# A message-passing layer on one core: another order of the step, slots found earlier, smaller last segments, the second bias by ScalarE

## The chip, the cores and the metric

The kernel runs on one core of one Trainium2 chip. The metric is the device time of one execution in microseconds (us). TensorE (PE) does matrix products, VectorE (DVE) and ScalarE (ACT) work elementwise, GpSimd (POOL) issues the indirect DMAs here, SyncE (SP) issues the plain ones. PSUM is the accumulator that TensorE writes, in banks of 128 partitions by 512 f32 words; SBUF is the on-chip memory; the tables named below lie in DRAM.

## The reference

`x` is 12500 nodes by 128 features. There are 412500 edges with a source, a target (sorted by target), 20 attributes and a weight.

```python
h    = relu(layernorm(x)) @ W_in2f
Wij  = (ssp(edge_attr @ W_f1 + b_f1) @ W_f2 + b_f2) * edge_weight[:, None]
agg  = segment_sum(h[dst] * Wij, src, 12500)
out  = x + ssp(agg @ W_o1 + b_o1) @ W_o2 + b_o2       # ssp(v) = softplus(v) - log 2
```

The edges are sorted by `dst`, so a run of edges reads few rows of h; the sum goes by `src`, which is in no order. That sum is what shapes the kernel.

## The kernel before, in words

**Chunks.** The edges are cut into 806 chunks of 512 (`CH`), each of four tiles of 128 (`QT`); four chunks make a group, 202 groups in all. For every chunk the kernel forms the 512 x 128 messages and POOL sends them by four indirect DMAs (one per tile, L795, "scatter") into rows ("slots") of a table in DRAM. The slots of a table are laid out by blocks of 128 source nodes (98 blocks), so that a later pass can load all messages of one block and add them up by products with a one-hot matrix. In each slot the 129th word is the node's place within its block.

**Slots.** Which slot an edge takes is its rank among the edges of its block so far. `blocks` (L673, VectorE) makes the one-hot of the blocks (128 x 392), `rank` (L692 and, to pass the count on, L725) multiplies it with a triangle of ones into one PSUM bank that is kept for this, `free`; `rank_end` takes the maximum over the blocks (`top`, L697, VectorE), and three small steps on VectorE make row numbers of it (L717 to L721). Ranks are made six chunks ahead of the chunk whose messages are sent (`LR` = 6).

**Messages.** For chunk k: SP loads the 32 rows of h that it reads (`rows`, table h3, three bf16 parts, tile `near`); VectorE makes the one-hot `at` (`window`, L744); TensorE multiplies them (`pick`, L772, into `picked`); ScalarE scales that by the edge weight (`picked`, L780, `hg`, four instructions). Beside it, for two chunks at a time, TensorE makes z = f W_f1 (`hidden`, L653), ScalarE Abs (L656), Exp (L657) and Ln (L662, `hidden_log`), and VectorE joins them to `r` (`hidden_end`, L668): that is the softplus. ScalarE copies the constant b_f1-and-b_f2 term into a PSUM bank (`bias`, L757), TensorE adds r W_f2 onto it in eight passes (`value`, L764, `v`). VectorE multiplies o = v hg (`message`, L791), and POOL scatters o. `v` and `picked` share three PSUM banks.

**Sums.** The groups are cut into segments (`SEGS` = 88, 40, 30, 14, 14, 8 and 8 groups), each with its own table. Once a segment's chunks are sent, `Collect` goes through its table in units of up to six tiles (`UT`): `load` by SP (tile `m`, L833), `compare` on VectorE (L844, one-hot `to`), `add` on TensorE (L857, into `acc`, a bank for four blocks, a "quad"), `keep` (L878 by ScalarE for the first segment, L880 by VectorE for the others, into `agg`, which stays in SBUF). With T tiles per block of 16, 8, 6, 3, 3, 2 and 2 (one more in a few blocks) that makes 4066 tiles in 824 units. All segments but the last are collected beside the chunks that follow; from the first segment's end (chunk 352) on, each step has some units, paced by planned due times (L995 to L1035).

**The order.** `step(k)` (L940 to L985) writes the order of each engine's work by hand, and no scheduler changes it. Its order for chunk k is: loads; blocks (k+7), end of the pair's softplus, window (k+2), message (k), keep; value and pick (k+1), bias (k+2), picked (k+1); compares; rank, hidden (k+4), log, add, tops. Clears of the slots (L1099, DMAs by SP) and the preparation of h (`make_h`, 25 quads of four node tiles) run beside the steps.

**Start and tail.** Ahead of the first chunk the kernel loads constants and makes h of the first four node tiles (`make_h(0)`), whose own table `tables[0]` serves the first chunks. After the last scatter come the rest of the units, the last segment's 206 tiles, and `finish` for each quad: z_out (L414), Abs and Relu (L385, L386), Exp and Ln (L394, L395), their sum (L420), x + b_o2 (L423), v_out (L427), the last add (L431) and the store (L434). The tail runs these parts of successive quads side by side.

Of the kernel before, what the change touches and what calls it, by code (L numbers as in the profile page):

```python
# [22 lines left out]
SEGS = (88, 40, 30, 14, 14, 8, 8)  # L23
# [6 lines left out]
UT = 6  # L30
# [6 lines left out]
def ceil_div(a, b):  # L37
    return -(-a // b)
# [3 lines left out]
def gnn_kernel(  # L42
# [38 lines left out]
    class Segment:  # L81
# [4 lines left out]
        def __init__(self, k):  # L86
# [7 lines left out]
            mean = (SEGS[k] * TG * P - (own[1] - own[0])) / QT * P / N  # L94
# [32 lines left out]


    tables = [(0, QN)]
# [4 lines left out]
    for c in range(NC):  # L134
        n = c * CH * N // n_edges
        table_of.append(0 if n < QN - NEAR - P else min(n // QN, NQ - 1) + 1)
# [4 lines left out]
    bf1, nbf1, bo1 = (sbuf(n, [P, 1]) for n in ("bf1", "nbf1", "bo1"))  # L141
# [10 lines left out]
    bf12 = sbuf("bf12", [P, P])  # L152
    zero = sbuf("zero", [P, ZR * RW])
# [27 lines left out]
    def load_x(q):  # L181
        n = min(QT, NTILE - q * QT)
        full = min(n, N // P - q * QT)
        xb = ln.tile([P, QT, P], F32, name="xb")
        if full < n:
            nc.vector.memset(xb[:, full:n, :], 0.0)
            nc.sync.dma_start(xb[:N % P, full, :], x[q * QN + full * P:N, :])
        if full:
            nc.sync.dma_start(xb[:, :full, :], x[q * QN:q * QN + full * P, :]
# [61 lines left out]

    def constants():
# [3 lines left out]
        first_load(0)  # L256
        nc.sync.dma_start(win, w_in2f)

        for j in range(NCHUNK):
            nc.sync.dma_start(wf1[32 * j:32 * j + RBF, :], w_f1)  # L260

        nc.scalar.preload_act_table_set("natural_log_exp_and_others")
        nc.scalar.dma_start(bf1, b_f1[:, None])
        nc.scalar.dma_start(wf2, w_f2)
        nc.scalar.dma_start(bf2, b_f2[None, :].to_broadcast([P, P]))
        make_identity(nc, ident)
        for _ in bounds(0, nc.gpsimd):
            pass

        prow_i = early_room[:WP, rows_at + 5 * NC:rows_at + 5 * NC + 1].bitcast(I32)  # L270
# [6 lines left out]
                                pattern=[[1, P]], channel_multiplier=-1)  # L277
        nc.gpsimd.memset(zero, 0.0)
# [8 lines left out]
        nc.vector.memset(bad, 0.0)  # L287
        nc.vector.memset(rel[:, NPART - 1, :], 0.0)
        nc.vector.memset(ones, 1.0)
        nc.vector.memset(none, 0.0)  # L290

        for t in range(QT):
            nc.vector.memset(turn[:, :, t:t + 1], -1.0 if t % 2 else 1.0)
        nc.vector.tensor_scalar(prow_i, prow_i, 7, None, op0=ALU.logical_shift_right)
        nc.vector.tensor_copy(prow, prow_i)
# [3 lines left out]

    def biases(psum):  # L300
# [911 lines left out]
```

## Time and profile before

| what | value |
|---|---|
| time, median of 13 runs | 5758.44 us (5727.84 to 5780.44) |
| the profiled execution's own time | 5751.31 us |
| its span | 5749.6 us |
| granted TensorE clock, mean | 0.726 of full speed |
| TensorE busy (weight loads) | 3837.9 us, 67% (2884.0 us, 50%) |
| VectorE busy | 3381.9 us, 59% |
| ScalarE busy | 2715.2 us, 47% |
| GpSimd busy | 3101.1 us, 54% |
| DMA | 820.80 MB, mean 143 GB/s |

By stage, from the busy time of each engine in three stretches:

| stretch, us | what runs | TensorE | VectorE | ScalarE | GpSimd | clock |
|---|---|---|---|---|---|---|
| 144 to 2416 | chunks alone | 1241 | 1152 | 1112 | 1282 | 0.62 |
| 2416 to 5608 | chunks and sums | 2387 | 2032 | 1466 | 1744 | 0.79 |
| 5608 to 5750 | sums and finish | 118 | 110 | 62 | 0 | 0.94 |

How to read the lines that follow. A group's line gives source line, engine, operation, the tiles it writes and reads, and a count; then busy us and the mean ns of one; then the engine's idle time just before these instructions, and what ended most of it. "issue" means that the profile shows nothing the engine waited for; "remote" that it was released by a semaphore whose sender the profile does not tell. A line of waits gives who waits for whom, the sum in us, the number of waits and the longest one (or, for issue, the sum, the count and the longest). A line of the timeline gives the start in us, the duration, engine, line, operation, tiles, and in brackets the idle time before it.

### The profile page before, as it was taken

To read this page: it belongs to the slowest core of one execution; us is meant where nothing else is said; L and a number is where in the kernel's file an instruction comes from. 1 tells how busy PE (TensorE), PEld (TensorE's weight loads), DVE (VectorE), ACT (ScalarE), POOL (GpSimd) and SP (SyncE) were. 2 spreads that over 40 slices of the span, in tenths; PEclk is the share of its full clock that TensorE was granted. 3 is DMA by queue.
4 is the path that set the end of the run, shared out by engine and by line. 5 is a ranking of instruction groups with operands and counts; after the bars stand their busy time and mean duration, and the time that the engine had idled before them with its cause. 6 is when DMAs were issued, how large, how long until landed. Compare 5 with 4: busy or idle time off the path is not lost. (4 is left out here: it accounts for less than half of the span.)

```text
span 5749.6 us, 71871 instructions
## 1 busy us (share of the span) xinstructions
PE 3837.9 (67%) x21576; PEld 2884.0 (50%) x21576; DVE 3381.9 (59%) x6726; ACT 2715.2 (47%) x5490; POOL 3101.1 (54%) x3244
## 2 busy tenths in 40 slices
PE   6555555655555555467777777777777777677778
PEld 4333333433333333356656566665656666555567
DVE  6555555555444444466665656666666666676767
ACT  5455555545444444444444444444444444444444
POOL 5555655655555555555555555555555555555550
PEclk7666666656665656678777778787877878787879
DMA  5444444443333333355664555655555556545547
GB/s 157 132 128 147 132 130 130 132 121 101 100 89 90 99 106 94 82 151 159 182 190 133 156 154 148 186 174 152 159 171 178 166 146 186 171 139 154 140 127 216
DMA packets 515581, 820.80 MB, mean 143 GB/s; under 512 B 177074, under 2 KB 312870, under 8 KB 515186
## 3 DMA queue, kind: packets, MB, share of 16 engines
q1 hardware_dynamic: 411586, 602.85, 37.4%
q0 software_dynamic: 103168, 213.15, 11.3%
q8 instruction: 176, 2.88, 0.2%
q14 instruction: 219, 1.79, 0.1%
q10 hardware_dynamic: 432, 0.13, 0.0%
HBM read 419.09 MB, written 396.64 MB: 142 GB/s over the span
## 5 line engine op out<-in xcount | busy, mean ns | idle before, releaser
L795 POOL DMA_INDIRECT slots<-o,slot x3224 | 3097.9, 961 | 2506.4 <-DVE o L791 1603.1
L764 PE MATMUL v<-wf,r 128*128 128x128 f32 x6448 | 1195.0, 342 | 561.8 <-issue 222.4
L857 PEld LDWEIGHTS acc<-to,m 128*128 128x128 f32 x8132 | 1237.8, 236 | 594.0 <-issue 281.8
L857 PE MATMUL acc<-to,m 128*128 128x128 f32 x8132 | 1332.1, 327 | 294.2 <-DVE agg L880 155.1
L780 ACT ACTIVATE hg<-picked,rcut 128x128 f32<-128x128 f32 x3224 | 913.0, 365 | 1276.1 <-remote 801.9
L764 PEld LDWEIGHTS v<-wf,r 128*128 128x128 f32 x6448 | 1066.4, 249 | 877.0 <-issue 332.0
L697 DVE TENSOR_REDUCE top<-free 128x4 f32<-128x392 f32 x806 | 451.3, 560 | 1622.4 <-remote 847.0
L757 ACT ACTIVATE v<-bf 128x512 f32<-128x512 f32 x804 | 478.1, 595 | 1196.6 <-DVE o L791 846.8
L653 PE MATMUL z<-f,wf 20*128 20x512 f32 x1612 | 654.6, 862 | 411.8 <-DVE r L668 238.0
L844 DVE TENSOR_TENSOR to<-count_ps,m 128x512 f32<-128x512 f32 (+3 forms) x824 | 644.6, 805 | 246.6 <-remote 111.3
L772 PE MATMUL picked<-near,at 96*128 96x128 bf16 x3224 | 391.6, 255 | 478.4 <-ACT hg L780 328.1
L668 DVE SCALAR_TENSOR_TENSOR r<-z,nbf,a 128x1024 f32<-128x1024 f32 x403 | 516.2, 1281 | 243.3 <-ACT a L662 128.4
L656 ACT ACTIVATE a<-z,bf 128x1024 f32<-128x1024 f32 x403 | 454.1, 1127 | 376.7 <-remote 282.4
L772 PEld LDWEIGHTS <-at 96*128 96x128 bf16 x3224 | 311.5, 117 | 540.5 <-issue 513.7
L791 DVE TENSOR_TENSOR o<-v,hg 128x512 f32<-128x512 f32 x806 | 547.8, 680 | 16.1 <-ACT hg L780 12.2
L744 DVE TENSOR_TENSOR at<-count_ps,rel 96x512 bf16<-96x512 f32 x806 | 545.3, 677 | 0.0
L653 PEld LDWEIGHTS z<-f,wf 20*128 20x128 f32 x1612 | 172.4, 236 | 629.2 <-issue 457.3
L662 ACT ACTIVATE a<-a,half 128x1024 f32<-128x1024 f32 x403 | 468.1, 1161 | 0.0
L673 DVE TENSOR_TENSOR inb<-count_ps,blk 128x392 f16<-128x392 f32 x806 | 445.7, 554 | 0.0
L657 ACT ACTIVATE a<-a 128x1024 f32<-128x1024 f32 x403 | 425.9, 1057 | 12.8
L725 PE MATMUL free<-inb,rest_of 128*128 128x392 f16 x806 | 331.9, 412 | 102.7 <-issue 53.8
L692 PE MATMUL free<-inb,after 128*128 128x392 f16 x806 | 330.4, 410 | 15.1 <-issue 7.8
(108 smaller groups left out, 1145.0 us busy)
## 6 DMA issues: line engine op xcount, KB each, us to landing
m<-slots SPq DMA_DIRECT2D x311, 387.0 KB
m<-slots SPq DMA_DIRECT2D x317, 258.0 KB
rel<-rel_d SPq DMA_DIRECT2D x202, 384.0 KB
m<-slots SPq DMA_DIRECT2D x172, 322.5 KB
slots<-o,slot POOLq DMA_INDIRECT x3224
slots<-zero SPq DMA_DIRECT2D x96, 387.0 KB
slots<-zero SPq DMA_DIRECT2D x64, 516.0 KB
f<-in_f_t SPq DMA_DIRECT2D x404, 80.0 KB
```

Of the source, the lines that this page charges most:

```text
L653: nc.tensor.matmul(z[:, k, :], wf1[rows, :], self.f[rows, :], start=True, stop=True)
L662: nc.scalar.activation(a, a, AF.Ln, bias=half, scale=0.5)
L668: nc.vector.scalar_tensor_tensor(r, z, nbf1, a, op0=ALU.max, op1=ALU.add)
L744: nc.vector.tensor_tensor(at, prow_ps.to_broadcast([WP, CH]), self.rel[:, c, :], op=ALU.is_equal)
L757: nc.scalar.activation(v, spread(bf12, QT), AF.Copy)
L764: nc.tensor.matmul(v[:, i, :], r[:, i * P:(i + 1) * P], wf2, start=False, stop=True, skip_group_check=True)
L772: nc.tensor.matmul(ps[:, i, :], at[:, i * P:(i + 1) * P], near, start=i == 0, stop=i == QT - 1, skip_group_check=True)
L780: nc.scalar.activation(hg[:, i, :], ps[:, i, :], AF.Copy, scale=self.rcut[:, j:j + 1])
L791: nc.vector.tensor_mul(o[:, :, :P], v, hg)
L795: put = nc.gpsimd.indirect_dma_start(out=views[j % VIEWS], out_offset=bass.IndirectOffsetOnAxis(ap=self.slot[:, j:j + 1], axis=0), in_=o[: ...
L844: nc.vector.tensor_tensor(to[:, :n, :], count_ps[:, None, :].to_broadcast([P, n, P]), self.m[u][:, :n, P:].to_broadcast([P, n, P]), op=ALU ...
L857: nc.tensor.matmul(self.acc[b // QT][:, i, :], m[:, j, :P], to[:, j, :], start=t == 0, stop=t == self.seg.tiles(b) - 1)
```

## The change

The order of the step and what feeds it are rewritten:

- **Step.** VectorE's part begins with message(k), then the tops of the rank before, blocks, end, window (now k+3), later the compares. TensorE's begins with pick (k+2), then value (k+1). `picked` has two banks of its own, `v` has one. The tops of a rank are taken a step after its product. Abs, Exp and Ln of a pair are issued together, a step after z.
- **Bias of v.** ScalarE's copy (L757) is gone; a fifth product, ones x (the constant in three bf16 parts), ends `value`.
- **Slots ahead.** `Group` is split in two: `Places` (slots, blocks, ranks) and `Group` (features, weights, h rows). Ranks run 6 chunks ahead up to chunk 100, then gain a chunk every two steps up to 110 (`LEAD`). When all ranks are made, the bank `free` becomes a second bank for sums.
- **Segments.** `SEGS` ends in 12, 8, 3, 3, 4 groups; T is 16, 8, 5, 4, 3, 2, 1, 1, 1, which makes 4182 tiles; units have up to four tiles (1202 units), the last segment 108 tiles. Nine buffers for `m`; `to` uses three tiles of `make_h`. The pace of the units is 1.5 times as high in the last 110 steps.
- **Start.** h of the first node tile is made alone, with a table of its own; constants are reordered over the queues and steps; slot clears start at step 12.
- **Finish.** The outputs' softplus takes Abs, Exp, Ln and one VectorE step (max and add) instead of two ScalarE passes and an add. ScalarE writes b_o2 (with the bias term of the max) into the bank of v_out, onto which the product is added; the add of b_o2 on VectorE is gone. z_out uses the two halves of one bank pair in turn; the last segment's loads run six units ahead.

The core of the diff:

```diff
-SEGS = (88, 40, 30, 14, 14, 8, 8)
+SEGS = (88, 41, 25, 18, 12, 8, 3, 3, 4)
+LEAD = 110
...
-UT = 6
+UT = 4
...
-    tables = [(0, QN)]
+    made_h = [(0, 1), (1, QT - 1)]
+    made_h += [(t, min(QT, NTILE - t)) for t in range(QT, NTILE, QT)]
+
+
+    tables = [(0, P), (0, QN)]
     for q in range(NQ):
         start = max(0, q * QN - NEAR)
         tables.append((start, (q + 1) * QN + NEAR + P - start))
     table_of = []
     for c in range(NC):
         n = c * CH * N // n_edges
-        table_of.append(0 if n < QN - NEAR - P else min(n // QN, NQ - 1) + 1)
+        table_of.append(0 if n <= P - 2 * WR else 1 if n < QN - P - WR
+                        else min(n // QN, NQ - 1) + 2)
...
+        seeded = z is not None
+        if z is None:
+            z = psum.tile([P, 2, CH], F32, name="z_out", tag="z")[:, 0, :]
+        for p, cs, rows in pieces:
+            xi = xo[:p, cs, :]
+            if not seeded:
+                nc.vector.tensor_add(xi, xi, spread(bo2[:p, :], xi.shape[1]))
+        z = z[:, :n * P]
         nc.tensor.matmul(z, wo1, sT, start=True, stop=True)
         a_n = quad.tile([P, 2, CH], F32, name="a_out", tag="a", bufs=2)[:, 0, :n * P]
         r_n = quad.tile([P, 2, CH], F32, name="r_out", tag="r", bufs=3)[:, 0, :n * P]
-        softplus_parts(a_n, r_n, z, bo1)
+        nc.scalar.activation(a_n, z, AF.Abs, bias=bo1)
         softplus_logs(a_n)
         yield
-        nc.vector.tensor_add(r_n, r_n, a_n)
-        for p, cs, rows in pieces:
-            xi = xo[:p, cs, :]
-            nc.vector.tensor_add(xi, xi, spread(bo2[:p, :], xi.shape[1]))
-        yield
-        v = psum.tile([P, QT, P], F32, name="v_out", tag="v", bufs=3)
+
+        nc.vector.scalar_tensor_tensor(r_n, z, nbo1, a_n, op0=ALU.max, op1=ALU.add)
+        yield
+        v = psum.tile([P, QT, P], F32, name="v_out", tag=tag, bufs=bufs)
+        if seeded:
+            nc.scalar.activation(v[:, :n, :], spread(bo2, n), AF.Copy)
         for i in range(n):
-            nc.tensor.matmul(v[:, i, :], r_n[:, i * P:(i + 1) * P], wo2, start=True, stop=True)
+            nc.tensor.matmul(v[:, i, :], r_n[:, i * P:(i + 1) * P], wo2, start=not seeded,
+                             stop=True, skip_group_check=seeded)
...
+        def rel_load(group):
+            g = group.g
+            if g == 0:
+                rel_store(0)
+            nc.sync.dma_start(group.rel, rel_d[g * NCHUNK:(g + 1) * NCHUNK, :][None, :, :]
+                              .to_broadcast([WP, NCHUNK, CH]))
+
...
+        class Places:
...
-                    self.slot = edge.tile([P, TG], I32, name="slot", bufs=4)
+                    self.slot = edge.tile([P, TG], I32, name="slot", bufs=LEAD // NCHUNK + 6)
...
+            def hidden_log(self, c):
+                z = self.pair[c]
+                a = quad.tile([P, 2, CH], F32, name="a", bufs=2)
+                nc.scalar.activation(a, z, AF.Abs, bias=bf1)
+                nc.scalar.activation(a, a, AF.Exp, scale=-1.0)
+                nc.scalar.activation(a, a, AF.Ln, bias=half, scale=0.5)
+                self.pair[c] = z, a
...
-            def bias(self, c):
-
-
-                v = psum.tile([P, QT, P], F32, name="v", bufs=3)
-                if self.g * NCHUNK + c < 2:
-                    nc.tensor.matmul(v.rearrange("p t f -> p (t f)"),
-                                     ones[0:1, :].to_broadcast([1, P]), spread(bf12[0:1, :], QT),
-                                     start=True, stop=False, skip_group_check=True)
-                else:
-                    nc.scalar.activation(v, spread(bf12, QT), AF.Copy)
-                return v
-
-            def value(self, c, v):
-
+            def value(self, c):
+
+                v = psum.tile([P, QT, P], F32, name="v", bufs=1)
                 r = self.pair[c // 2 * 2][:, c % 2, :]
                 for i in range(QT):
                     nc.tensor.matmul(v[:, i, :], r[:, i * P:(i + 1) * P], wf2,
-                                     start=False, stop=True, skip_group_check=True)
+                                     start=i == 0, stop=False, skip_group_check=True)
+                nc.tensor.matmul(v.rearrange("p t f -> p (t f)"), ones_b, spread(bf12_p, QT),
+                                 start=False, stop=True, skip_group_check=True)
                 return v
 
-            def pick(self, c, at, ps):
-
+            def pick(self, c, at):
+
+                ps = psum.tile([P, QT, P], F32, name="picked", bufs=2)
                 near = self.near.pop(c)
                 for i in range(QT):
                     nc.tensor.matmul(ps[:, i, :], at[:, i * P:(i + 1) * P], near,
                                      start=i == 0, stop=i == QT - 1, skip_group_check=True)
+                return ps
...
+        def sums_tile():
+
+            kept["banks"] = kept.get("banks", 0) + (made["rank"] == NCH - 1 and not ranked)
+            if kept["banks"] % 2:
+                return state_ps.tile([P, QT, P], F32, name="acc_b", tag="free")
+            return psum.tile([P, QT, P], F32, name="acc")
...
-                m = edge.tile([P, UT, RW], F32, name="m", bufs=5)
+                m = edge.tile([P, UT, RW], F32, name="m", bufs=9)
...
-                to = edge.tile([P, UT, P], F32, name="to", bufs=3)
+                kept["to"] = kept.get("to", 0) + 1
+
+                to = ln.tile([P, UT, P], F32, name="to", tag=("xb", "xT", "left")[kept["to"] % 3])
...
+        def served():
+
+            for c in range(NCH):
+                start, rows = tables[table_of[c]]
+                if stored[0] < min(NTILE, ceil_div(start + rows, P)):
+                    return c - 1
+            return NCH
+
...
+        RAMP = 20
+        LEAD_AT = 100
+        LATE = NCH - LEAD
...
+        def ahead(k):
+
+            lead = LR if k < LEAD_AT else min(LR + (k - LEAD_AT) // 2, LEAD)
+            return min(k + lead, k + 1 + (k + 1) * (LR - 1) // RAMP, NCH - 1)
...
+            steady = k >= RAMP
+            late = k >= LATE
+            part("rows", min(k + LW, 2 * k + 3, served()), rows)
             group((k + LG) // NCHUNK)
-            part("rows", min(k + LW, 2 * k + 3, NEXT if k < NEXT - 3 else NCH), rows)
-            for c, u in units:
-                c.load(u + AHEAD)
-
-            part("blocks", min(k + LR + 1, 2 * k + 1), blocks)
-            part("end", min(k + LZ - 2, made.get("log", -1)), pairs(hidden_end))
-            part("window", k + 2 if k > 0 else k + 1, window)
+            slots_of((ahead(k) + LG) // NCHUNK)
+
+            def keep():
+                for c in owed:
+                    c.keep()
+                owed.clear()
+
+            def slots():
+                for r in ranked:
+                    next(r, None)
+                ranked.clear()
+
+            def rank():
+                made["rank"] += 1
+                ranked.append(ranks(made["rank"]))
+                next(ranked[0])
+
+            def add(most):
+
+                while len(summed) > most:
+                    c, u = summed.pop(0)
+                    c.add(u)
+
+            def waiting():
+
+                return late and summed and summed[0][0].seg.T == 1
+
+
+            if not steady:
+                slots()
             if has(k):
                 g, c = of(k)
                 g.message(c, vs.pop(k), hgs.pop(k))
-            for c in owed:
-                c.keep()
-            owed.clear()
+            keep()
+            if steady:
+                slots()
+                if ahead(k) > made["rank"] + 1:
+                    rank()
+            else:
+                part("window", k + 1 + max(0, k) * 2 // (RAMP - 2), window)
+            if waiting():
+                add(2)
+            part("blocks", made["rank"] + 2, blocks, place)
+            part("end", min(k + LZ - 2, made["log"]), pairs(hidden_end))
+            keep()
+            if steady:
+                part("window", k + 3, window)
+
+            while not steady and made["rank"] < ahead(k):
+                slots()
+                rank()
+            part("pick", k + 1 if k < RAMP - 2 else k + 2, pick)
             if has(k + 1):
                 g, c = of(k + 1)
-                vs[k + 1] = g.value(c, bs.pop(k + 1))
-                ps = psum.tile([P, QT, P], F32, name="picked", tag="v", bufs=3)
-                g.pick(c, ats.pop(k + 1), ps)
-            if has(k + 2):
-
-                bs[k + 2] = of(k + 2)[0].bias(of(k + 2)[1])
+                vs[k + 1] = g.value(c)
+            if waiting():
+                add(1)
+            for seg, u in units:
+                seg.load(u + AHEAD)
+
             if has(k + 1):
-                hgs[k + 1] = g.picked(c, ps)
+                hgs[k + 1] = g.picked(c, ps.pop(k + 1))
+
+            for _ in range(2 if k == 0 else k < 5):
+                next(h[1], None)
+            part("log", min(k + LZ - 1, made["hidden"]), pairs(hidden_log))
+
+            keep()
             for c, u in units:
                 c.compare(u)
-            upto = max(made["rank"], min(k + LR, 2 * k + 1))
-            ready = [ranks(j) for j in range(made["rank"] + 1, upto + 1)]
-            made["rank"] = upto
-            for r in ready[:1]:
-                next(r, None)
+                summed.append((c, u))
+            while made["rank"] < ahead(k):
+                slots()
+                rank()
             part("hidden", k + LZ, pairs(hidden))
-            part("log", k + LZ - 1, pairs(hidden_log))
-            for c, u in units:
-                if summed:
-                    summed[0].add(summed[1])
-                summed[:] = c, u
-            for r in ready:
-                for _ in r:
-                    pass
+            if k < 4:
+                part("log", k + LZ, pairs(hidden_log))
+            if units:
+                add(len(units) if waiting() and units[-1][0].seg.T == 1 else 1)
...
+        def pace(k):
+            return k + 0.5 * max(0, k - LATE)
...
+            zs = psum.tile([P, 2, CH], F32, name="z_out", tag="z")
...
+                tag = ("picked", 2) if b // QT % 3 else ("v", 1)
+                outs.append(finish(b, n, sT, quad, psum, *tag, z=zs[:, b // QT % 2, :]))
...
-                last.load(u + AHEAD)
+                last.load(u + 2 * AHEAD)
```

## The prediction

> **What bounds the kernel now.** I read the costliest groups first, then the list of waits, then one stretch of the timeline, then the tail. The group that fills the span is the scatter:
>
> ```profile
> L795 POOL DMA_INDIRECT slots<-o,slot x3224 | 3097.9, 961 | 2506.4 <-DVE o L791 1603.1
> ```
>
> The times after the bar are busy us, mean ns and the idle time before it. POOL's row alone adds up to the whole execution: 3097.9 busy + 2506.4 idle before scatters + 141.4 after the last one (its end at 5608.2, span 5749.6) + 3.9 of start. The list of waits splits the idle time:
>
> ```profile
> POOL slots L795 <- DVE o L791: 1603.1, 366, 25.4
> POOL slots L795 <- issue: 883.1, 2798, 2.0
> DVE top L697 <- remote: 847.0, 141, 11.7
> ACT hg L780 <- remote: 801.9, 147, 8.0
> ```
>
> The 883.1 are gaps of 0.30 us between scatters; four scatters of 0.961 + 0.30 make 5.05 us a chunk, which nothing in the change touches (806 x 5.05 = 4070). What can be won is the 1603.1, of which 25.4 is the start: 1578 us in 365 waits, 4.3 us each, always for the product o, never for a slot. "remote" on DVE and ACT is the other half of the story. The timeline of one cycle shows it:
>
> ```profile
> 1583.42 0.53 PE L692 MATMUL free<-inb,after 128*128 128x392 f16 x1
> ...
> 1590.83 0.96 POOL L795 DMA_INDIRECT slots<-o,slot  x1 [0.30 <-issue]
> 1594.53 1.14 ACT L780 ACTIVATE hg<-picked,rcut 128x128 f32<-128x128 f32 x4 [5.82 <-remote]
> 1594.57 0.57 DVE L697 TENSOR_REDUCE top<-free 128x4 f32<-128x392 f32 x1 [10.54 <-remote]
> ...
> 1595.67 0.56 DVE L673 TENSOR_TENSOR inb<-count_ps,blk 128x392 f16<-128x392 f32 x1
> ...
> 1596.74 1.28 DVE L668 SCALAR_TENSOR_TENSOR r<-z,nbf,a 128x1024 f32<-128x1024 f32 x1 [0.51 <-ACT a L662]
> 1597.94 0.68 DVE L744 TENSOR_TENSOR at<-count_ps,rel 96x512 bf16<-96x512 f32 x1
> ...
> 1598.61 0.68 DVE L791 TENSOR_TENSOR o<-v,hg 128x512 f32<-128x512 f32 x1
> ...
> 1599.56 0.96 POOL L795 DMA_INDIRECT slots<-o,slot  x1 [7.77 <-DVE o L791]
> ```
>
> TensorE issued the matmul of L692 at 1583.42, but VectorE, idle, could start on its result only at 1594.57. The answers of TensorE come late while scatters run back to back, and come 2.7 us after the last one ended (1591.8). Then VectorE works 4.1 us through its queue (top, three slot steps, blocks, end, window) before o, and POOL starts 0.95 us after o starts. In this part the cycle repeats about every 27.8 us with four chunks: 20.1 busy, 7.7 lost. So a wait has two parts: TensorE's late answer, and VectorE's queue ahead of o. Taken chunk by chunk from the rows of L780, L791 and L795 (gaps over 0.6 us):
> - chunks 20 to 351 (no sums collected): 118 gaps, 612.7 us; in 297.8 of them hg was finished and o was not started. 6.81 us a chunk.
> - chunks 352 to 805: 256 gaps, 968.6 us (3.8 each, one per 1.77 chunks); 557.0 with hg finished. 7.02 us a chunk.
>
> **Part by part.**
>
> *Hand-overs.* In the new order VectorE's step begins with message (o), then top, blocks, end, window, compares; pick runs two chunks ahead of message, so hg is ready a step earlier, and o waits only for value (v). The 4.1 us of queue go behind o. Next late is v itself: it has one bank, so value(k+1) waits for o(k) and o(k+1) for value(k+1). That chain is 2.08 (value's eight passes at half clock, L764) + about 0.5 (new bias matmul) + 0.68 (o) + 0.2 of hand-overs = 3.5 us, under POOL's 5.05. Queued behind a waiting value on TensorE: the rank matmuls, z and the sums; who waits for those is VectorE's top, ACT's Abs and the sums' bank, all a step later. In the cycle shown TensorE answers promptly from 1594.5 to about 1606, 11.5 us, which is three turns of 3.5. A cycle is then three chunks (15.1) + the late answer (2.7) + o (0.95) = 18.8, or 6.25 us a chunk; two chunks would give 6.9, four 5.95. Since 11.5 us is barely three turns, I let one cycle in four end at two chunks: (3 x 18.8 + 13.75) / 11 = 6.38, and 332 x (6.81 - 6.38) = **-143**. In the second stage a gap keeps 3.78 - 2.18 = 1.6 us (557.0 / 256 = 2.18). Gaps that are shorter come oftener; with one every 1.2 chunks instead of 1.77 that is 5.05 + 1.33 = 6.4.
>
> *Bias by a matmul, not by ACT.* 804 x 0.595 = 478 us leave ACT (47% busy, so only order counts). TensorE gets 806 matmuls of 512 columns and their weight loads. The trace has none in bf16: bounds are L692 (392 columns, 0.33 to 0.53) and L653 (512 in f32, two passes, 0.59 to 1.2 each); near the first, I take 0.5.
>
> *Segments and UT 4.* From the sizes: 4066 tiles (two passes each: the 8132 of L857's row) become 4182, 824 compares 1202. By the forms of L844 (384 columns 0.549, 768 columns 0.948) a unit costs 0.15 + 0.133 a tile: 378 x 0.15 + 116 x 0.133 = 72 us, and 50 more adds of 0.68 = 34; 0.24 us a chunk on VectorE in the second stage, which is 64% busy there (2032 of 3192). With the bias that leaves VectorE near 4.7 and TensorE (2387 of 3192, so 5.3) near 5.8 us a chunk; I add 0.1 a chunk for it: 454 x (7.02 - 6.5) = **-236**.
>
> *Slots 110 chunks ahead.* No wait names a slot, so this alone gives nothing. Between chunks 100 and 308 it adds half a rank a chunk (L697 0.56 + L673 0.55 on VectorE, L692 + L725 0.82 on TensorE, half of each): hidden, since both engines are near half busy there. The last 110 chunks have none, take half more collecting per chunk, and have a second bank for sums; I count these as even. SP issues some 380 more, smaller loads, ahead of near's; near was issued 24 to 56 us before its pick (1300 to 1660 us), so nothing shows.
>
> *Start.* The first scatter is at 29.4 us: hg(0) was finished at 22.2, but o waited to 28.4 behind L668, which waited for the next pair's Ln. With message first and one tile of 128 rows normalised instead of four (statistics 1.7 us, scaling 1.1), I take 21: **-8**; between 0 and -12.
>
> *Tail.* From 5640.7 to 5743.9, 25 quads at 4.1 us, TensorE 95 of 103 us busy: 16 passes of 0.12 + z 1.02 + v 1.05 = 4.0. With one tile a block it is eight passes: 3.05. VectorE, as full today (compares 1.38, L880, L420, L423 and L431 0.68 each: 4.1), keeps one compare of 512 columns, the sum, one softplus step and the last add, 4 x 0.68 = 2.7; ACT has 0.69 + 0.63 + 0.72 + 0.60 = 2.64. 25 x 0.95 = 24, and some 11 of the 32 us of older sums ahead of it: **-35**.
>
> Sum: 5751.3 (this execution's own time, span 5749.6; the median 5758.4 of 13 runs is 0.1% above it) - 8 - 143 - 236 - 35 = 5329; I say **5330 us**.
>
> [...]
>
> **Rivals.**
> 1. *Three queues really come apart.* All of the 855 us (297.8 + 557.0) go, with no shorter bursts: 5751 - 855 - 43 = 4850. For it: 5.95 a chunk is still over POOL's 5.05. Against: TensorE's late answers remain.
> 2. *The wait refills.* TensorE's answers are tied to POOL's pauses; if only two chunks fit between pauses, the loop stays at 6.8 to 7.0 and only start and tail are won: 5710. For it: hg and top wait 801.9 and 847.0 for "remote", and none of that is in VectorE's order.
> 3. *Slower: the single bank of v.* Every chunk needs an answer of TensorE between two o's, where v and picked shared three banks. If that answer is late by more than 3.4 us in the mean (5.05 + 1.8 of today, less the chain's 3.5), the loop is longer than now; at 4.3 us it is 7.7 a chunk: 786 x 0.9 = +700 less 43, so 6400; I put the case at 5800 to 6400. For it: L692's answer took 10.5 us above. Against: the late answers come in bursts, between which they take 0.04 us.
> 4. *Moved, not won:* VectorE meets o with compares still unfinished in the second stage (4.7 of 6.5), and only the first stage, start and tail gain: 5751 - 143 - 43 = 5565. I keep it inside the forecast's range.
>
> **How the numbers follow.** Forecast (5050 to 5600) 0.60, at 5330; rival 1 (under 5050) 0.08; rival 2 (5600 to 5735) 0.20; rival 3 0.10; no change 0.02. The range takes in rival 2 and leaves out rivals 1 and 3 and no change, together 0.2: 5050 to 5720. Faster by over 0.3% (17 us, about what can be told from no change): 0.88; within: 0.02; slower: 0.10.
>
> **What would show it.** Right: POOL's wait for o falls from 1603 to 1100 to 1300 us, o starts within 1 us of hg and v in most gaps, first scatter near 21, tail near 106, ACT down by some 480. If the idle before o stays at 1600 and hangs on TensorE's v, rival 2 holds; if gaps are more and longer with v named, rival 3. Wrong altogether: POOL's gaps of 0.30 or its 0.961 change.

## The result and the profile after

The changed kernel takes 5380.88 us (median of 10 runs, 5372.89 to 5394.88) beside 5751.03 us for the kernel before (46 runs): a ratio of 0.9357, 95% interval 0.934 to 0.9373. The profiled execution took 5388.36 us, span 5386.6 us, 363.0 us less than the span before. The forecast was 5330, range 5050 to 5720.

The costliest groups of the page after; the columns are those of before:

```profile
L859 POOL DMA_INDIRECT slots<-o,slot x3224 | 3096.5, 960 | 2082.1 <-DVE o L855 1186.3
L824 PE MATMUL v<-wf,r 128*128 128x128 f32 x6448 | 1196.4, 343 | 514.2 <-DVE o L855 482.4
...
L855 DVE TENSOR_TENSOR o<-v,hg 128x512 f32<-128x512 f32 x806 | 552.8, 686 | 1336.8 <-remote 715.6
```

and its list of waits:

```profile
POOL slots L859 <- DVE o L855: 1186.3, 429, 16.6
POOL slots L859 <- issue: 871.0, 2750, 1.6
DVE o L855 <- remote: 715.6, 176, 8.8
...
ACT hg L844 <- remote: 385.0, 85, 11.7
```

The scatters cost what they did (960 ns, 0.30 us apart). Their wait for o fell from 1603.1 to 1186.3 us, spread over more and shorter gaps (429 for 366). Before, o itself hardly waited (16.1 us idle before it); now VectorE stands idle 1336.8 us before o, mostly for "remote". The waits of top have gone from the head of the list. One stretch of the timeline shows what is left:

```profile
1508.05 0.96 POOL L859 DMA_INDIRECT slots<-o,slot  x1 [0.30 <-issue]
1508.16 0.38 PE L826 MATMUL v<-bf_p,ones_b 128*128 128x512 bf16 x1
...
1509.31 0.95 POOL L859 DMA_INDIRECT slots<-o,slot  x1 [0.30 <-issue]
...
1512.13 0.69 DVE L855 TENSOR_TENSOR o<-v,hg 128x512 f32<-128x512 f32 x1 [4.34 <-remote]
...
1513.09 0.96 POOL L859 DMA_INDIRECT slots<-o,slot  x1 [2.83 <-DVE o L855]
```

The last product of v was issued at 1508.16; VectorE, idle for 4.34 us, started o at 1512.13, 1.9 us after POOL's last scatter ended. In this stretch no queue stands ahead of o any more: the late answer of TensorE is the whole wait. It is not so everywhere. In chunks 20 to 351 VectorE stood idle for over 1 us on a late v in 124 of the 155 gaps (329 of 406 us). In chunks 352 to 805 this holds for 167 of 312 gaps (419 of 787 us); in 144 others VectorE came to o from other work, mostly the sums' compares, after it had itself waited for a sum.

By stage, from the starts of the scatters (four scatters with their pauses make a floor of 5.05 us a chunk):

| | before | after | change | forecast |
|---|---|---|---|---|
| first scatter, us | 29.4 | 21.7 | -7.7 | -8 |
| chunks 0 to 19, us | 127.4 | 131.4 | +4.0 | 0 |
| chunks 20 to 351, us a chunk | 6.81 | 6.16 | -216 us | -143 |
| chunks 352 to 805, us a chunk | 7.03 | 6.58 | -205 us | -236 |
| from the last scatter's end, us | 141.4 | 203.0 | +61.6 | -35 |

In chunks 20 to 351 the gaps of over 0.6 us went from 118 of 5.19 us to 155 of 2.62 us; o now starts 1.65 us after the last scatter ended instead of 4.24.

The tail went the other way. A piece of it after:

```profile
5264.73 1.16 PE L467 MATMUL v_out<-wo,r_out 128*128 128x128 f32 x8 [2.68 <-ACT v_out L465]
...
5267.01 1.91 PE L454 MATMUL z_out<-agg,wo 128*128 128x512 f32 x2
...
5268.96 0.69 ACT L457 ACTIVATE a_out<-z_out,bo 128x512 f32<-128x512 f32 x1 [4.29 <-PE z_out L454]
...
5270.97 0.58 ACT L465 ACTIVATE v_out<-bo 128x512 f32<-128x512 f32 x1
...
5271.61 1.16 PE L467 MATMUL v_out<-wo,r_out 128*128 128x128 f32 x8 [2.68 <-ACT v_out L465]
```

From one quad's v_out to the next it takes 6.7 us in the mean (7.1 in the median) where it took 3.7; the prediction's 4.1 divides a stretch of 103 us by 25 quads. ScalarE's write of b_o2 (L465) is issued behind Abs, Exp and Ln of the quad two later. TensorE waits with v_out for that write, and only after v_out come the next sums and the next z_out, on which ScalarE's next softplus waits: a ring through two engines.

### The profile page after: what moved, and what is told of

Its sections match the earlier page's. It is cut to its first block, busy times and chain, and to the rows that moved or that the text cites. A ratio compares the mean times of both kernels' runs of the same rounds, so it can differ in the third digit from the quotient of the medians.

```text
span 5386.6 us, 75521 instructions
## 1 busy us (share of the span) xinstructions
PE 3878.7 (72%) x22612; PEld 2888.8 (54%) x22612; DVE 3447.9 (64%) x7238; ACT 2338.3 (43%) x4695; POOL 3100.6 (58%) x3250
## 4 chain that ended last, share of the span: by engine, by line
## 5 line engine op out<-in xcount | busy, mean ns | idle before, releaser
L859 POOL DMA_INDIRECT slots<-o,slot x3224 | 3096.5, 960 | 2082.1 <-DVE o L855 1186.3
L844 ACT ACTIVATE hg<-picked,rcut 128x128 f32<-128x128 f32 x3224 | 902.4, 370 | 1364.3 <-remote 385.0
L855 DVE TENSOR_TENSOR o<-v,hg 128x512 f32<-128x512 f32 x806 | 552.8, 686 | 1336.8 <-remote 715.6
L824 PEld LDWEIGHTS v<-wf,r 128*128 128x128 f32 x6448 | 1045.8, 246 | 572.3 <-DVE o L855 521.7
L931 PEld LDWEIGHTS acc<-to,m 128*128 128x128 f32 x6940 | 973.7, 218 | 363.0 <-issue 297.9
L931 PE MATMUL acc<-to,m 128*128 128x128 f32 x6940 | 1052.6, 308 | 142.4 <-issue 110.7
L793 PE MATMUL z<-f,wf 20*128 20x512 f32 x1612 | 569.9, 786 | 198.3 <-issue 109.8
L918 DVE TENSOR_TENSOR to<-count_ps,m 128x512 f32<-128x512 f32 (+2 forms) x1202 | 675.2, 608 | 32.0 <-DMA m<-slots 13.4
L835 PEld LDWEIGHTS <-at 96*128 96x128 bf16 x3224 | 288.2, 113 | 283.0 <-issue 198.1
L835 PE MATMUL picked<-near,at 96*128 96x128 bf16 x3224 | 379.4, 248 | 60.1 <-issue 32.7
L694 PEld LDWEIGHTS <-after 128*128 128x128 f16 x806 | 92.6, 115 | 578.4 <-issue 535.2
L826 PE MATMUL v<-bf_p,ones_b 128*128 128x512 bf16 x806 | 380.4, 472 | 1.0 <-issue 1.0
L793 PEld LDWEIGHTS z<-f,wf 20*128 20x128 f32 x1612 | 149.9, 226 | 392.3 <-issue 264.8
```

Of the source, the lines that this page charges most:

```text
L793: nc.tensor.matmul(z[:, k, :], wf1[rows, :], self.f[rows, :], start=True, stop=True)
L824: nc.tensor.matmul(v[:, i, :], r[:, i * P:(i + 1) * P], wf2, start=i == 0, stop=False, skip_group_check=True)
L835: nc.tensor.matmul(ps[:, i, :], at[:, i * P:(i + 1) * P], near, start=i == 0, stop=i == QT - 1, skip_group_check=True)
L844: nc.scalar.activation(hg[:, i, :], ps[:, i, :], AF.Copy, scale=self.rcut[:, j:j + 1])
L855: nc.vector.tensor_mul(o[:, :, :P], v, hg)
L859: put = nc.gpsimd.indirect_dma_start(out=views[j % VIEWS], out_offset=bass.IndirectOffsetOnAxis(ap=places_of[self.g].slot[:, j:j + 1], axi ...
```

## The experiments

The first eight kernels, e1 to e8, ran on two chips, where the kernel before took 5755.2 and 5750.7 us. The last four, e9 to e12, ran on a third chip, where **the kernel before took 4231.35 us** (15 runs); a ratio holds for the chip it was measured on.

### e1: the product first, nothing else

```diff
 def step(k):          # the kernel before
+    message(k); keep
     blocks; end; window
-    message(k); keep
     value, pick (k+1); bias (k+2); picked (k+1)
```

> The kernel before with one edit: in step(k) the product o = v hg (message) is VectorE's first instruction, ahead of blocks, end of the softplus and window. Everything else stays: picked one chunk ahead, bias by ScalarE, v and picked on three shared banks. Theory A (half of POOL's wait is VectorE's queue ahead of o: 3.2 us of o after hg per gap in chunks 20 to 351, 2.9 after that): the mean gap falls from 5.2 to about 3.3 us and from 3.8 to about 2.6 us, gaps come somewhat oftener, time 5400 to 5580. Rival B (order alone is worth little, because hg is still made in the same step from an answer of TensorE; it is the pick two chunks ahead with banks of its own that counts): 5650 to 5760.

5568.27 us, ratio 0.9672 (0.9643 to 0.9701): 187 of the change's 370 us. Its waits:

```profile
POOL slots L795 <- DVE o L791: 1433.5, 373, 19.3
ACT hg L780 <- remote: 890.4, 156, 8.7
POOL slots L795 <- issue: 876.8, 2812, 1.5
DVE top L697 <- remote: 867.8, 147, 9.8
```

In the gaps o now starts 0.8 to 1.6 us after hg instead of about 3, so VectorE's queue is gone as A said. The time lies in A's range, the gaps do not: in chunks 20 to 351 the mean gap is 3.8 us where A wanted 3.3, and a chunk falls from 6.81 to 6.42 us; after that the mean gap stays at 3.6 where A wanted 2.6, and a chunk falls only from 7.03 to 6.91. There hg is the late one, and ScalarE waits longer for its answer (890.4 for 801.9). The first scatter comes at 23.3 us, so the order alone makes 6.1 of the 7.7 us of the start.

### e2: slots six chunks ahead

```diff
-LEAD = 110
+LEAD = 6
```

> The changed kernel with LEAD = 6 instead of 110: slots are found six chunks ahead to the end, no second bank for sums, no faster pace at the end. Theory A (no wait ever named a slot, so the lead is worth nothing by itself; in the last 110 chunks half a rank more per chunk against a lower pace of sums is even): 5350 to 5430. Rival (the lead is what made the loop faster): chunks 20 to 695 go from 6.2 to 6.5 us back towards 6.8 to 7.0, time 5550 to 5750.

5409.19 us, ratio 0.9396 (0.9368 to 0.9424). As A expected, the lead with all that hangs on it is worth 28 us, and not in the loop but behind it, where the tail grows from 203.0 to 240.8 us without it; the edit also takes away the faster pace and the second bank, and which of them counts was not taken apart. In the loop the lead costs time: in chunks 100 to 307, where it is built up, a chunk takes 6.08 us here and 6.17 to 6.19 in the changed kernel, e4, e6 and e7, whose ranks run alike. That is some 20 us; ahead of these chunks the kernels agree (6.11 beside 6.08 to 6.13).

### e3: two banks for v, one for picked

```diff
-v = psum.tile([P, QT, P], F32, name="v", bufs=1)
+v = psum.tile([P, QT, P], F32, name="v", bufs=2)
-ps = psum.tile([P, QT, P], F32, name="picked", bufs=2)
+ps = psum.tile([P, QT, P], F32, name="picked", bufs=1)
```

> The changed kernel with two banks for v and one for picked instead of one and two. What is left of POOL's wait is v: in chunks 20 to 695 o starts 3.5 to 4.8 us after the last pass of v was issued, with VectorE idle for 2.3 to 3.4 us. Theory A (TensorE's answers are late as long as scatters run back to back, whenever the question was put): two banks ask 0.7 us earlier but the answer comes with POOL's pause; gaps stay at 2.3 to 2.7 us, time 5340 to 5420. Rival (the single bank of v is what makes v late: value waits for o 482 us in all): the gaps go, 5050 to 5250. A third outcome: the single bank of picked makes hg late again, and the loop loses: above 5450.

5435.29 us, ratio 0.9443 (0.9414 to 0.9472), between A's range and the third outcome's. The gaps did not shrink (2.62 us in chunks 20 to 351 and 2.57 in 352 to 695, beside 2.62 and 2.30), as A said. Hg was finished some 8 us before o in them, so it is still v that is late, and its single bank is not the cause. In its place TensorE waits 355.3 us for ScalarE to clear picked's single bank, and the last scatter ends 44 us later.

### e4: the write of b_o2 one part earlier

```diff
 nc.vector.scalar_tensor_tensor(r_n, z, nbo1, a_n, op0=ALU.max, op1=ALU.add)
-yield
 v = psum.tile([P, QT, P], F32, name="v_out", tag=tag, bufs=bufs)
 if seeded:
     nc.scalar.activation(v[:, :n, :], spread(bo2, n), AF.Copy)
+yield
```

> The changed kernel with ScalarE's write of b_o2 into the bank of v_out issued one part earlier in finish, together with the step that makes r_out, so that it no longer stands on ScalarE behind Abs, Exp and Ln of the quad two later. Theory A (after the last scatter each quad takes 7.0 us because TensorE's v_out waits for this write, which waits on ScalarE for the softplus of a later quad's z_out, which TensorE can only make after v_out): the quads fall to 3.1 to 4.1 us, the tail from 203 to 105 to 130 us, time 5285 to 5310. Rival (the chain runs through the sums, agg and z_out, and the write only happens to lie in it): the tail stays within 20 us of 203, time 5360 to 5390.

5297.61 us, ratio 0.9198 (0.917 to 0.9226). Theory A holds: 3.1 us a quad, tail 124.3 us. TensorE's wait in the tail, of the kernel before, then of the changed kernel and of this one:

```profile
L427 PE MATMUL v_out<-wo,r_out 128*128 128x128 f32 x196 | 26.1, 275 | 0.9 <-DVE r_out L420 0.9
```

```profile
L467 PE MATMUL v_out<-wo,r_out 128*128 128x128 f32 x196 | 38.5, 358 | 61.4 <-ACT v_out L465 61.0 <-DVE r_out L461 0.4
```

```profile
L467 PE MATMUL v_out<-wo,r_out 128*128 128x128 f32 x196 | 28.1, 288 | 1.1 <-ACT v_out L464 1.1
```

61.0 us of waiting became 1.1. The passes themselves shortened too (358 to 288 ns), while the granted clock of this stretch rose from 0.79 to 0.94.

### e5: one scatter in four

```diff
-for i in range(QT):
+for i in range(QT if self.seg is segs[0] else 1):
...
-return max(0, int(m - 5 * m ** 0.5)) // ZR * ZR
+return max(0, int(m - 5 * m ** 0.5)) // ZR * ZR if k == 0 else 0
```

> The changed kernel in which, from chunk 352 on, POOL sends only the first of the four tiles of each chunk, and the slots of these segments are all cleared: three quarters of the messages of chunks 352 to 805 are left out of the sums; every product and every load stays. Chunks 0 to 351 are untouched (6.1 to 6.2 us each). Theory A (TensorE's answers are late because scatters run back to back): from chunk 352 on VectorE's and ScalarE's waits of over 1 us for answers of TensorE vanish, and the chunk costs what TensorE and VectorE have to do, 5.1 (862 us busy in 168 chunks) to 5.8 us instead of 6.43; time 4950 to 5130. Rival (the answers are late on their own, with the changes of the granted clock or because of the loads): 6.2 to 6.5 us a chunk, time 5300 to 5400.

4598.66 us (one run), faster than A's own range. From chunk 352 on, a chunk takes 4.84 us. The two stretches, this kernel's and then the changed kernel's (from and to, length, then busy us and number of instructions of TensorE, its weight loads, VectorE, ScalarE and GpSimd; then clock, DMA share, GB/s):

```profile
2194.00:4391.00 2197.00, 2016.94 (x15482) 1674.70 (x15481) 1996.39 (x4001) 1249.30 (x2506) 433.07 (x453) 0.96 0.70 211
```

```profile
2197.00:5184.00 2987.00, 2375.34 (x15516) 1901.83 (x15516) 2021.89 (x4010) 1255.83 (x2509) 1739.01 (x1816) 0.86 0.61 179
```

The same work of TensorE, VectorE and ScalarE takes 2197 us instead of 2987. Answers of v that kept an idle VectorE over 1 us: 170 in this part of the changed kernel, one here. In chunks 20 to 351, where the scatters are all there, they are 142 in both kernels. So on these chips the late answers come with the scatters, as theory A says, though its price was too high: it wanted 5.1 to 5.8 us a chunk. The 4.84 us, what all but three of four scatters needs at this stretch's clock of 0.96, lies just under POOL's 5.05. Whether it is POOL's issuing or the transfers themselves that make the answers late, the edit can't tell: it takes away both.

### e6: the segments of before

```diff
-SEGS = (88, 41, 25, 18, 12, 8, 3, 3, 4)
+SEGS = (88, 40, 30, 14, 14, 8, 8)
```

> The changed kernel with the segments of before (88, 40, 30, 14, 14, 8, 8) and units of four tiles. The last segment has 206 tiles again, 16 passes for each quad instead of 8. Theory (the small last segments are worth only the tail's passes, since the tail's quads are a chain in which the sums are one link): chunks 352 to 805 within 20 us of the changed kernel's, tail 20 to 45 us longer, time 5390 to 5430. Rival (the sizes are what moved the loop, by fewer or smaller loads): chunks 352 to 805 slower by 100 us or more, above 5480.

5323.93 us, ratio 0.9261 (0.9224 to 0.9298): outside both. It is 57 us faster than the changed kernel: the last scatter ends 44 us earlier (24 of them in the last 110 chunks, 6.79 for 7.01 us each), and 33 to 38 us earlier than in e4 and e7, whose loops are the changed kernel's. The tail is no longer (200.9) although the last segment has twice the tiles: the ring of the tail covers its passes. As long as the ring is there, the new sizes cost time.

### e7: b_o2 by VectorE again

```diff
-seeded = z is not None
+seeded = False
```

> The changed kernel with b_o2 added to x by VectorE again, and nothing written by ScalarE into the bank of v_out. By the theory that e4_seed bears out (v_out waits for a write that stands behind a later quad's softplus on ScalarE), the quads fall from 7.0 to 3.4 to 4.2 us (VectorE has five instructions of 0.68 for each): tail 115 to 130 us, 5285 to 5320. If the tail stays above 180 us, the chain is another one, and e4_seed was faster for another reason.

5295.86 us, ratio 0.9211 (0.9174 to 0.9248), as expected: tail 122.8 us, 3.3 us a quad in the mean. ScalarE's write is worth nothing in either place; in the place where the change put it, it costs some 85 us.

### e8: a chunk further ahead

```diff
 # on top of e4
-part("pick", k + 2); value(k + 1)
+part("pick", k + 2); value(k + 2)           # v and picked with two banks each
-count_ps, prow_ps = counts[:, :P], counts[:WP, P:]     # a PSUM bank
+count_ps, prow_ps = places, prow                        # SBUF
```

> e4_seed (measured at 5297.6) with TensorE's answers asked for a whole chunk earlier: value runs two chunks ahead of message as pick does, v and picked have two banks each, the softplus runs a step earlier; the eighth bank comes from the constants that the one-hots are compared with, which VectorE now reads from SBUF. Theory A1 (single answers are 4 to 8 us late, each for itself): one chunk more (5.05 us) covers most of them, the loop falls from 6.16 and 6.45 to 5.3 to 5.8 us a chunk, time 4750 to 4950. Theory A2 (answers come only when POOL pauses): a cycle holds one chunk more for the same pause, 2.6 us in 3.1 chunks instead of 2.1: 5.9 and 6.1 to 6.2, time 5020 to 5120. Rival (the loop is bound elsewhere, or the compares from SBUF cost VectorE or POOL time): 5290 or more.

5546.19 us, ratio 0.9653 (0.961 to 0.9696): the rival's side, 249 us slower than without. Gaps became fewer and longer: in chunks 20 to 351 from 152 of 2.64 us to 91 of 4.7, nearly the same sum for a chunk (1.2 and 1.3 us); in chunks 352 to 805 from 304 to 111, and the sum from 1.7 to 1.1 us a chunk, which is what A2 wanted there, though with longer pauses (4.4 us) and not, as A2 had it, with the same. Single waits of ScalarE for an answer reach 28 us. What outweighs it is a second effect, which e11 takes apart: a scatter takes 1102 ns here instead of 963, in the mean 0.56 us more for each chunk (0.2 in chunks 20 to 351, 0.8 after them).

### e9: both edits that had gained

```diff
 # on top of e4
-SEGS = (88, 41, 25, 18, 12, 8, 3, 3, 4)
+SEGS = (88, 40, 30, 14, 14, 8, 8)
```

> e4_seed with the segments of before (units of four tiles): the two edits that each made the changed kernel faster (5297.6 and 5323.9 against 5380.9). If they are independent, 5297.6 + 5323.9 - 5380.9 = 5240. If the last segment's 16 passes a quad, which the slow chain of the tail had covered in e6_segs, show once that chain is gone (4.0 instead of 3.1 us a quad), some 25 us come back: 5260 to 5290.

On the third chip: 4229.97 us, ratio to the kernel before 0.9996 (0.9986 to 1.0005). The expected microseconds can't be compared with it. The profile tells why it is so short (the first line is POOL's busy share in 40 slices of the span, in tenths):

```profile
POOL 6777777777777777777777777777777777777760
...
L859 POOL DMA_INDIRECT slots<-o,slot x3224 | 3095.5, 960 | 1003.0 <-issue 766.1
```

The scatter is as long as on the other chips (960 ns) and POOL has no gap over 0.6 us after chunk 20: 5.05 to 5.07 us a chunk to the end. Not one late answer of v is there (142 and 170 in the changed kernel on the first chips). The kernel before was not profiled on this chip, but its time says that it runs at that floor too: its first scatter and tail on the other chips and 806 chunks of 5.05 make 29.4 + 4070 + 141.4 = 4241, measured 4231. So the change's gain in the loop is the repair of a wait that this chip does not show. One part of the expectation can be read here: with the ring gone the last segment's 16 passes do show, 4.0 us a quad and a tail of 123.0 us, beside 3.1 us and 104.5 to 115.5 in e10 to e12.

### e10: a chunk further ahead, constants left in PSUM

```diff
 # as e8, but
-count_ps, prow_ps = places, prow
+count_ps, prow_ps = counts[:, :P], counts[:WP, P:]
-v bufs=2, picked bufs=2; hg (k+1)
+v bufs=2, picked bufs=1; hg (k+2), three buffers
```

> e4_seed (5297.6) with value and hg two chunks ahead, as e8_deep, but with the compares' constants left in PSUM: v has two banks, picked one. Theory A (in e8_deep the depth did shorten POOL's waits, to 1.1 us a chunk from 1.7 in chunks 352 to 805, and the loss came from scatters of 1.10 us in place of 0.96): scatters at 0.96, chunks 352 to 805 at 5.9 to 6.2 us, time 5050 to 5200. Rival B (late answers only get longer when more is asked ahead, 26 us at most in e8_deep, and the single bank of picked gives back what the second of v gains, as in e3_v2): 5280 to 5400.

Third chip: 4265.86 us, ratio 1.0085 (1.0068 to 1.0102). With no late answers there, it says nothing on A or B. It has 15 gaps (47.5 us) soon after the sums begin, in chunks 390 to 438. The single bank of picked is not seen to make them: hg was finished over 5 us before o in all 15, TensorE waits for that bank 3.6 us in the whole run, and what VectorE had waited for in them was mostly the product of the next rank (32 us), which on TensorE stands behind sums, pick and value. What depth does where answers are late stays open.

### e11: constants in SBUF, nothing else

```diff
 # on top of e4
-count_ps, prow_ps = counts[:, :P], counts[:WP, P:]
+count_ps, prow_ps = places, prow
```

> e4_seed (5297.6) with one edit: VectorE's compares read their constant (node numbers, 128 x 128, and row numbers) from SBUF instead of PSUM; TensorE's order and all banks as in e4_seed. Theory (compares that read only SBUF slow POOL's scatters): a scatter takes 1.05 to 1.15 us instead of 0.96, POOL's busy time is 3400 to 3600 us, time 5400 to 5600. Rival (the scatters of 1.10 us in e8_deep came from its depth): 0.96, 5285 to 5310.

Third chip, 4666.57 us (one run):

```profile
L858 POOL DMA_INDIRECT slots<-o,slot x3224 | 3554.2, 1102 | 1001.0 <-issue 803.8 <-DMA slots<-o,slot 77.1 <-DVE o L854 31.6
```

1102 ns and 3554 us, as the theory said, where e9, e10 and e12 have 960 ns on the same chip; e8 has the same 1102 ns on another. VectorE's compares take what they did (window 681 for 677 ns, one-hot of the blocks 556 for 556): only POOL pays. The loop runs at 5.38 us a chunk and, with the sums' compares, at 5.7 to 5.9, with no gap over 0.6 us: the floor itself has risen.

### e12: the bias of v by ScalarE

```diff
 # on top of e4
+nc.scalar.activation(v, spread(bf12_f, QT), AF.Copy)
...
-nc.tensor.matmul(v, ones_b, spread(bf12_p, QT), start=False, stop=True)
```

> e4_seed (5297.6) with the bias of v written by ScalarE again, into the single bank of v ahead of the eight passes, instead of the fifth product. Theory A (the product only replaces 478 us of ScalarE, which is not full; what it adds to the chain from o over v to o is 0.595 - 0.47 us and a hand-over, and the chain stays under POOL's 5.05): 5300 to 5380. Rival (ScalarE's write, which must wait for o, holds up hg behind it, and this was a main part of what the change gained): 5420 or more.

Third chip: 4243.67 us, ratio 1.0033 (1.0021 to 1.0046). Beside e9's 0.9996 it loses 14 us. The two differ in the segments as well, but these touch the first 20 chunks little, and there e12 loses 18 us (6.17 for 5.25 us each); after that POOL runs at its floor with either, and the smaller last segment gives some 7 back in the tail. What the product is worth where answers are late was not measured.

## Why the prediction was right, and where it was not

**What bounds the kernel: right.** POOL's row is the account: with the wait gone (e9, third chip) the loop runs at 5.05 to 5.07 us, the floor, and with three of four scatters gone (e5) the rest needs 4.84.

**Hand-overs: the mechanism right, the sizes off both ways.** Message first took VectorE's queue away, as e1 shows alone, and the late answer stayed. The prediction's cycle was three chunks, one time in four two, and a gap of 3.65 us; measured are 2.1 chunks (332 chunks, 155 gaps) and 2.62 us. It took the answer to come 2.7 us after the last scatter; o starts 1.65 us after it, and in 27 of the 142 late answers before that end or within 0.3 us of it. Its sum also counts the 0.30 us of issue that lie in each gap twice; without that it gives 6.27 us. Measured is 6.16: the term was -216, not -143. That o would follow v within 1 us was wrong: in 153 of the 155 gaps it did not, and it follows 4.8 us after v's last product in the mean; the lateness moved from hg and top onto v.

**Second stage: near by luck.** -205 for -236. The term took gaps of 1.6 us, one in 1.2 chunks; measured are 2.52 us and one in 1.46. The 1.6 came from the 557.0 us of hg finished and o not started, but that figure also counts time in which the last scatter still ran: within the gaps it is 433 us (257 for the 297.8 of the first stage), and a gap would have kept 2.1. The 0.30 counted twice works the other way. VectorE's queue ahead of o is not gone here as it is in the first stage: in 144 of 312 gaps VectorE came from other work. The 0.1 us a chunk allowed for more tiles and units, 45 us, is about what the sizes of the segments alone cost (e6: 33 to 44 us); what the smaller units cost was not measured. The last 110 chunks, counted as even, stand at 7.01 us beside 6.44 ahead of them.

**Slots 110 chunks ahead: right** that the lead gains nothing in the loop. But the half rank a chunk more was not hidden, though both engines are near half busy there: it costs some 20 us in chunks 100 to 307 (e2). And it missed that the lead, with pace and bank, gives 38 us behind the loop.

**Bias: right in size.** 0.472 us for the product where 0.5 was taken. ScalarE's 478 us row is gone, but its busy time fell by 377 and not by the 480 forecast: the row overlaps others, and without it the trace of before has 418 us less.

**Start: right**, 21.7 for 21; the first 20 chunks then take 4 us more.

**Tail: wrong, and this is the step that failed.** It summed each engine's work and took the fullest one: "With one tile a block it is eight passes: 3.05". The passes do cost that (e4: 3.1 us a quad), but the order of the two queues made a ring of 7.1 us. The sum saw ScalarE's 2.64 us; it did not ask what stands ahead of L465 on ScalarE, and who waits for it. Even with the ring opened (e4) the tail is only 17 us shorter than before: quads at 3.1 for 3.7 us are worth 14 and not 24, the first v_out comes 10 us earlier, and what follows the last one takes 7 us more. +62 for -35 is an error of 97 us. That the sum of 5329 still met 5388 is luck in part: the loop with its first chunks gave 38 us more than forecast.

**The clock** rose: the granted clock was 0.795 in the mean where it had been 0.726, and 0.86 for 0.79 in chunks 352 to 805. **Rivals.** The first, that all of the 855 us go, fell to TensorE's late answers, as its own counter-argument had it: the loop gained 421. The second, that the wait refills, is true of message first alone in the second stage (e1: 6.91), not of the whole change. The third's mechanism, TensorE's answer between two o's, is what is left of the wait, but at about 2.6 us a gap and not on every chunk; the bank is not its cause (e3). The fourth, that VectorE meets o with compares unfinished, is seen in the 144 gaps above (367 us); the stage still gained 205.

## What stays open

Why TensorE's answers are late on two chips and not on the third is not settled. That they come with the scatters is shown (e5: 170 to 1). They come mostly while the granted clock is at 1.0: v's last product was issued at 1.0 in 97 of the 142, where it is so in 130 of all 332 chunks. But that is no proof of a cause, and on the third chip (e9) the clock is higher in the mean (0.87) and changes nearly as often (209 stretches in the first 1800 us beside 227) without one late answer. Only the half of the gain that message first brings (e1) was measured by itself. The rest of the loop's gain, 6.42 to 6.16 us and 6.91 to 6.58 us a chunk, comes with pick two chunks ahead, the banks, the bias product and the new order of the softplus together; the waits of hg (801.9 to 385.0) point to pick, but no run shows it alone. The changed kernel itself was not run on the third chip. From e9's end of the last scatter there (4103.5) and the changed kernel's tail (203.0) one would estimate 4307 us, slower than before by some 75; that is an estimate over two chips. Of the kernels that beat the changed one, e4 and e7 (5297.6 and 5295.9) are the fastest measured where answers are late; e4 with the old segments was measured only on the third chip.

## What to carry to other kernels

Where two engines' queues are written by hand, a stage's time is not the fullest engine's sum: follow each instruction to what stands ahead of it on its own queue and to who waits for it, and look for a ring. Put the instruction that feeds the bottleneck first in its queue; that one move was half of this gain (187 of 370 us). And before a wait is engineered away, find out on a second chip that it is there.

## What the runs showed of the hardware

- **Late answers.** On two chips VectorE and ScalarE, idle, start up to 12.0 us (28 us in e8) after the TensorE pass that they wait for was issued, while POOL issues indirect scatters of 0.96 us at 0.30 us distance. With a quarter of the scatters this is all but gone (e5: one late answer of v for 170); on a third chip there is none with all of them (e9), and the kernel before takes 26% less time (4231 for 5751 us).
- **Two operands in SBUF.** With the compares' constants in SBUF, where their other operand lies too, POOL's scatters took 1102 ns in the mean (e8, e11); with the constants in PSUM they took 963 (e4) and 960 (e9, on e11's chip). VectorE's own compares took 681 for 677 ns (window) and 556 for 556 (one-hot of the blocks). What lengthens the scatters no run shows.
- **The clock.** In the records of the kernel before and of the changed one the granted clock is 0.5 or 1.0, in stretches that are multiples of 3.41 us (3.41, 6.83, 10.24 and longer, but for the last of each run). Its mean in the tail was 0.79 in the changed kernel and 0.94 with the ring opened (e4).
